# A four-layer graph network on one core: projections and sort moved beside the attention heads, searches and layer joins rearranged

## The chip, the core and the metric

The kernel runs on one core of a Trainium2 chip. A core has a matrix engine (PE, TensorE), a vector engine (DVE), an activation engine (ACT), a general-purpose engine (POOL, GpSimd) and a queue engine (SP) that issues most DMA transfers. The metric is the device time of one execution in microseconds (us). Three runs of the kernel before took 3139.11, 3139.2 and 3142.6 us; the median is 3139.2.

## The reference

There are 2708 nodes with 128 features each, and one adjacency matrix of 2708 x 2708 with random weights (each entry is present with probability 0.00148, the diagonal always). Four layers follow one another, each as `x = x + layer(relu(layernorm(x)))`:

```
layer 0: d = sum(adj, axis=1);  s = 1/(sqrt(d)+1e-8)
         (adj * s[:,None] * s[None,:]) @ (h @ W + b)
layer 1: q,k,v = (h @ W.T).reshape(128, n, 8)        # 128 heads of width 8
         a = softmax(q k^T * 128**-0.5 + 2*adj);  (a v).reshape(n, 1024) @ Wo.T
layer 2: (adj.T @ h / deg) @ Wn.T + bn + h @ Wc.T + bc, batch norm, relu
layer 3: g[i,j] = sigmoid(a[j] + b[i] + b1) * adj[i,j]
         (sum_j g[i,j] * h[i]) @ weight + bias       # a, b = h @ w1 halves
```

The reshape of layer 1 is plain: head `d` is made of consecutive pieces of the flat (n x 1024) projection, so one head covers only about 21 nodes' projections.

## The kernel before

The nodes lie in 22 row tiles of 128 rows (the last has 20). Features stay in `x_sb` through all layers.

**Layer 0 (L258 to L530)** is written in a manual schedule, that is, each engine issues in the order of the source. The three projection weights are loaded and turned first (`weight_turned`). Then come the norm of all 22 tiles, transposes into `hT`, and `fc = h @ W + b`, where the bias enters by a second matmul against a row of ones. Two passes over the adjacency follow. A row tile is loaded, ACT sums it for the degree, DVE makes `dinv` and scales `fc` (L394 to L396), PE turns 128 x 128 blocks, and PE accumulates `l_s`. The first pass (L383 to L402) goes over all tiles and finishes 8 row tiles (`stay`); the second (L493 to L518) goes over the 14 others (`gone`).

Beside both passes runs a **search** per row tile, the generator `neighbours` (L129 to L176), advanced a step at a time by `look`. It finds the 16 largest entries of each row with their columns: 8 largest in each of five segments (DVE, L134, L138), the top 16 of these 40, then a one-hot table of 16 x 40 = 640 elements (`n_hot`, DVE), its product with the column numbers (POOL, L166) and its sum over 40 (`n_col`, DVE, L174). One search is finished before the next begins. Ten tiles are searched in the first pass (`early`), twelve in the second.

**Projection and sort (L629 to L671)** form a stage of their own. Per row tile PE makes six matmuls of 128 x 512 (`qkv_ps`, six PSUM buffers), ACT and DVE copy them out in turns with a scale, and SP stores 1.6 MB to `qkv_d`. Beside it the generator `in_order` (L569) sorts the nodes by their number of neighbours: a counting sort on DVE and PE, then 22 indirect scatters on POOL (L621) that write the sorted list to `list_d`, each ordered behind the one before it. `load_wo` then loads and turns the output weight.

**The heads (L731 to L1459)** treat the softmax by an expansion in features of q and k (81 combinations), so that a head's attention is a product of moments. Heads are prepared in groups of four (`prepare`: load of `raw` from `qkv_d`, a re-ordered copy stored for the neighbour phases). The main loop (L1399 to L1445) goes over 128 heads with 6 chunks of 3 or 4 row tiles. In each chunk: `turn` transposes the next chunk's query features (PE `f_ps`, copied by ACT to `fT`), `evaluate` multiplies (PE `g_ps`), DVE makes `z` and reduces it to `o_raw`; beside it the next head's query features (`fq`, `bq`, DVE), the key features two heads ahead (`fk`, `bk`, `y`, POOL) and the next head's moments (PE `m_ps`, then `mw` on DVE, L1278) are made. All PE instructions of a chunk stand in this order in PE's queue. A further generator, `first`, advances beside the chunks through three phases: `by_node`, `sorted_rows` (which reads `list_d`) and `from_neighbours` (exact terms of the neighbours). When it is done, `normalise` and `project_out` take its turns.

**Layer 2 (L1456 to L1616)** first makes a row of inverse degrees for all partitions (`di`, then 22 pairs of a diagonal tile, a matmul `d_ps` and a copy into `diB`, L1479 to L1488). Fallback loops that run zero times here follow, then the aggregation (`pg`, L1582), batch norm and its application, which takes DVE, ACT and 22 transposes.

**Layer 3 (L1619 to L1806)** does a norm over all tiles (`norm_relu`), 22 matmuls `ab_ps` with a bias matmul each, stores the tables `gate_d` and `own_d`, and has three loops for nodes with more than 16 neighbours, which run zero times here. The gather over 22 sorted tiles ends the kernel: indirect loads on POOL (L1661), sigmoid, products, output.

## Time and profile before

| what | value |
|---|---|
| median of the runs | 3139.2 us |
| profiled execution | 3144.25 us |
| its span | 3142.5 us (1.75 us lie around it) |
| mean granted PE clock | 0.895 |
| busy share: PE, DVE, POOL, ACT | 82%, 69%, 64%, 41% |
| norm and fc | 0 to 72 us |
| first pass, second pass of layer 0 | 72 to 211, 211 to 379.7 us |
| projection and sort, until the first moments of a head | 379.7 to 539.2 us |
| heads, with their tail | 539.2 to 2661 us |
| layer 2 | 2661 to 2808.5 us |
| join of layer 2 and 3 | 2808.5 to 2896 us |
| gather | 2896 to 3142 us |

In a line of groups the columns are source line, engine, operation, output and inputs, shapes, count; then busy time and the mean nanoseconds of one; then how long the engine stood idle just before and what ended that. In a timeline line the first two numbers are start and length in us. A matmul in 32-bit floats shows as two PE instructions. A share of busy time over the whole span mixes stages, so the stretches are read one by one.

### The profile page before, as it was taken

How to read it: one execution, taken by the hardware profiler on the slowest of the kernel's cores; microseconds unless marked ns; L12 is line 12 of the kernel's file. 1: busy time of each engine (PE TensorE's matmuls, PEld its weight loads, DVE VectorE, ACT ScalarE, POOL GpSimd, SP SyncE). 2: the span in 40 equal slices, each digit the busy share in tenths (PEclk: the TensorE clock that was granted, in tenths of full speed). 3: DMA queues.
4: the chain of work that ended last, by engine and by line, in shares of the span. 5: the costliest groups of instructions: out<-in, count | busy, mean ns of one | idle time of the engine just before them, and what ended most of it. 6: DMA issues, size and time to landing. Idle time of an engine off the chain costs nothing. (4 is left out here: it accounts for less than half of the span.)

```text
span 3142.5 us, 49745 instructions
## 1 busy us (share of the span) xinstructions
PE 2587.8 (82%) x17997; PEld 2225.8 (71%) x17997; DVE 2180.7 (69%) x5130; ACT 1297.9 (41%) x3165; POOL 2009.5 (64%) x2264
## 2 busy tenths in 40 slices
PE   6478796899889999999999999999989997785144
PEld 4377543888888888888888888888889886333133
DVE  3868743777778888888888888888788885222232
ACT  3577332566644444444444444444444442112010
POOL 0211114666678988989999898989777771001775
PEclk6689897999999999999999999999999998885555
DMA  3463174778743333333433443444366642632332
GB/s 110 173 237 125 49 316 182 229 240 247 217 144 115 134 131 121 138 136 135 141 131 139 143 142 135 148 142 143 84 159 167 163 123 80 233 110 84 90 87 63
DMA packets 309521, 462.50 MB, mean 147 GB/s; under 512 B 153774, under 2 KB 229488, under 8 KB 284178
## 3 DMA queue, kind: packets, MB, share of 16 engines
q1 hardware_dynamic: 277658, 290.28, 28.8%
q0 software_dynamic: 31600, 168.86, 15.6%
q8 instruction: 147, 2.41, 0.3%
q14 instruction: 116, 0.95, 0.1%
HBM read 344.49 MB, written 114.59 MB: 146 GB/s over the span
## 5 line engine op out<-in xcount | busy, mean ns | idle before, releaser
L1306 PE MATMUL g_ps<-mw,fT 128*128 128x128 f32 x5632 | 776.0, 280 | 28.8 <-DVE mw L1278 24.8
L1296 ACT COPY fT<-f_ps 128x512 f32<-128x512 f32 (+1 forms) x768 | 419.3, 546 | 869.7 <-PE f_ps L1294 867.1
L1268 PE MATMUL m_ps<-y,fk 123*128 123x128 f32 (+1 forms) x5632 | 754.2, 280 | 0.0
L1306 PEld LDWEIGHTS g_ps<-mw,fT 128*128 128x128 f32 x5632 | 706.6, 196 | 36.5 <-DVE mw L1278 30.5
L1268 PEld LDWEIGHTS m_ps<-y,fk 123*128 123x128 f32 (+1 forms) x5632 | 703.2, 197 | 0.0
L1216 POOL TENSOR_TENSOR y<-bk,raw 128x792 f32<-128x792 f32 x256 | 415.8, 1625 | 301.4 <-ACT y L1249 291.9
L1314 DVE TENSOR_TENSOR z<-g_ps,bq 128x324 f32<-128x324 f32 (+1 forms) x768 | 355.2, 462 | 293.8 <-PE g_ps L1306 293.6
L1294 PE MATMUL f_ps<-ident,fq 128*128 128x128 f32 x2816 | 451.9, 280 | 124.7 <-DVE v_sum L860 69.7
L1294 PEld LDWEIGHTS f_ps<-ident,fq 128*128 128x128 f32 x2816 | 336.0, 143 | 214.9 <-DVE v_sum L860 73.3
L1320 DVE TENSOR_REDUCE o_raw<-z 128x36 f32<-128x324 f32 (+1 forms) x768 | 355.8, 463 | 26.4
L1216 POOL TENSOR_TENSOR fk<-bk,raw 128x352 f32<-128x352 f32 (+1 forms) x384 | 356.3, 950 | 0.1
L1216 POOL TENSOR_TENSOR fk<-raw,bk 128x352 f32<-128x352 f32 (+1 forms) x512 | 311.7, 636 | 2.9 <-ACT bk L764 2.2
L1213 DVE TENSOR_TENSOR fq<-bq,kq_ps 128x528 f32<-128x528 f32 (+1 forms) x512 | 288.1, 605 | 0.0
L972 POOL TENSOR_TENSOR c_z<-c_kv,c_q 128x1024 f32<-128x1024 f32 (+1 forms) x121 | 284.1, 2348 | 2.0 <-DMA c_kv<-kv_n,srt 1.3
L1013 PE MATMUL v_ps<-c_v,ident 128*128 128x512 f32 (+1 forms) x484 | 228.8, 595 | 6.2 <-ACT c_acc L1028 6.2
L1661 POOL DMA_INDIRECT g<-gate_d,srt x121 | 121.7, 1006 | 109.7 <-issue 109.4
L1213 DVE TENSOR_TENSOR fq<-kq_ps,bq 128x352 f32<-128x352 f32 (+1 forms) x512 | 171.9, 378 | 0.0
L155 POOL CAST n_fl<-n_ci 128x40 f32<-128x40 int32 (+1 forms) x22 | 4.8, 216 | 252.1 <-DVE n_ci L138 252.1
L978 DVE TENSOR_REDUCE c_c<-c_z 128x128 f32<-128x1024 f32 (+1 forms) x121 | 147.5, 1219 | 3.1 <-POOL c_z L972 3.1
L996 DVE TENSOR_TENSOR c_v<-c_kv,c_c 128x1024 f32<-128x1024 f32 (+1 forms) x121 | 146.7, 1212 | 0.0
L1249 ACT COPY y<-raw 128x99 f32<-128x99 f32 x256 | 95.7, 375 | 108.4 <-PE m_ps L1268 106.8
L957 POOL DMA_INDIRECT c_kv<-kv_n,srt x121 | 117.5, 971 | 22.0 <-issue 15.0
(301 smaller groups left out, 3661.1 us busy)
## 6 DMA issues: line engine op xcount, KB each, us to landing
a_nat<-in_adj_dram SPq DMA_DIRECT2D x34, 1354.0 KB
raw<-qkv_d SPq DMA_DIRECT2D x128, 275.0 KB
n_raw<-qkv_d SPq DMA_DIRECT2D x128, 275.0 KB
qkv_d<-qkv SPq DMA_DIRECT2D x21, 1600.0 KB
a<-in_adj_dram SPq DMA_DIRECT2D x21, 1354.0 KB
kv_n<-n_kv SPq DMA_DIRECT2D x16, 1408.0 KB
o_g<-o_raw SPq DMA_DIRECT2D x31, 396.0 KB
q_n<-n_q SPq DMA_DIRECT2D x16, 704.0 KB
```

Of the source, the lines that this page charges most:

```text
L972: nc.gpsimd.tensor_tensor(zs[b][:sz], kvs[b][:sz, 0, :, 0], qs[t][:sz], ALU.mult)
L978: nc.vector.reduce_sum(cs[b][:sz], zs.pop(b)[:sz], axis=AX.X)
L996: nc.vector.tensor_tensor(z[:sz], kv[:sz, 0, :, 1].rearrange("p (j c) k -> p j c k", j=2), c.rearrange("p (j c) -> p j c", j=2)[:, :, :, None]
L1013: nc.tensor.matmul(accs[t][:sz, j], ident[:sz, :sz], z[:sz, j].rearrange("p c k -> p (c k)"), start=s0 == 0, stop=s0 == ROOM[t] - 1,)
L1213: nc.vector.tensor_tensor(o, x, y, ALU.mult)
L1216: nc.gpsimd.tensor_tensor(o, x, y, ALU.mult)
L1268: nc.tensor.matmul(pms[d][:, :P], fks[d][:sz, t], ys[d, h][:sz, m * VW * B_ALL : m * VW * B_ALL + P], start=t == 0, stop=t == NT - 1,)
L1294: nc.tensor.transpose(pt[:, m], fqs[d][:, t0 + m], ident)
L1296: nc.scalar.copy(fts[d, c][:, :n], pt[:, :n])
L1306: nc.tensor.matmul(pg[:, m], ft[:, m], mws[d], start=True, stop=True,)
L1314: nc.vector.tensor_tensor(z[:, :n], pg[:, :n, : B_ALL * VW].rearrange("p t (k b) -> p t k b", k=VW), bqs[d % 2][:, t0 : t0 + n, None, :B_A ...
L1320: nc.vector.reduce_sum(ros[g][:, t0 : t0 + n, i], z[:, :n], axis=AX.X,)
```

## The change

1. **Search.** POOL adds three halving sums (320, 160 and 80 elements), so that `n_col` on DVE reduces 5 instead of 40 per neighbour. `look` may let a second search step while the first waits for its table. `early` has 12 tiles instead of 10; the searches of two tiles begin beside the norm, one step per group of four tiles. `fc` is scaled by `dinv` on POOL instead of DVE. The bias of `fc` is added by DVE, four tiles at a time. The weights are turned between the two passes and interleaved per head, with the scale folded in.
2. **Projection.** The stage is gone. `projections` makes two row tiles (8 pieces of 32 heads) before the first head, and one piece per chunk of the first 13 and a third heads: two matmuls of 128 x 384 into one PSUM tile `v_ps` of two banks (a pool with one buffer), half of it copied by ACT and half by DVE into one of two buffers, and a store of 400 KB.
3. **Sort.** `in_order` follows in the same generator, one step per chunk, with one scatter per step. `sorted_rows` waits until it is done. Its tables and the tiles of the neighbour phases lie in `area`, where the weights were. The output weight is loaded later.
4. **Layer 2.** The inverse degrees are made after layer 0, stored, and loaded to all partitions by one broadcast transfer.
5. **Layer 2 to 3.** Batch norm's application, norm, matmul and table stores go by columns of four row tiles, several columns at different steps; batch norm is one ACT instruction per column; the bias is added by DVE. The three loops become one loop that holds the others.

```diff
@@ neighbours
+        w = CAND
+        while w > SEG:
+            w //= 2
+            nc.gpsimd.tensor_tensor(
+                hot[:sz, :, :w], hot[:sz, :, :w], hot[:sz, :, w : 2 * w], ALU.add
+            )
         yield
         col = pool.tile([P, KS], FP, name="n_col")
-        nc.vector.reduce_sum(col[:sz], hot[:sz], axis=AX.X)
+        nc.vector.reduce_sum(col[:sz], hot[:sz, :, :SEG], axis=AX.X)
@@ layer 0
-            early = stay + gone[:2]
-            wT = [weight_turned(w, f"wT{i}") for i, w in enumerate((wq, wk, wv))]
+            early = stay + gone[STAY - 1 :: 2]
...
+            def look(n):
+                for _ in range(n):
+                    while found:
+                        e = found[0]
+                        if len(found) > 1 and e[1] >= 3 and e[2] and found[1][1] < 3:
+                            e[2] = False
+                            e = found[1]
+                        else:
+                            e[2] = True
+                        e[1] += 1
+                        if next(e[0], "done") != "done":
+                            break
+                        found.remove(e)
+            begun_with = [order[0], order[2]]
+            for t in begun_with:
+                i = order.index(t)
+                found.append([neighbours(t, rows[t][1], nat[i], np_, seg0, at48), 0, False])
...
-                nc.tensor.matmul(pf[:sz], ones[0:1, :sz], b0_sb, start=False, stop=True)
-                nc.scalar.copy(fc[:sz, t], pf[:sz])
+                        nc.vector.tensor_tensor(
+                            fc[:sz, t0 + a : t0 + b],
+                            pf[:sz, a:b],
+                            b0_sb[:sz, None].to_broadcast([sz, b - a, C]),
+                            ALU.add,
+                        )
+                look(1)
...
-                nc.vector.tensor_scalar_mul(fc[:sz, t], fc[:sz, t], d)
+                nc.gpsimd.tensor_scalar_mul(fc[:sz, t], fc[:sz, t], d)
...
             products(len(ready))
+            for e, (w, scale) in enumerate(((wq, C**-0.5), (wk, 1.0), (wv, 1.0))):
+                weight_turned(w, f"w{e}", e, scale)
@@ after layer 0
+    di_d = dram.tile([N, 1], FP, name="di_d")
+    di = keep.tile([P, NT, 1], FP, name="di")
...
+    store_rows(nc.sync, di_d, di)
@@ in_order
-            if t % 2:
-                yield
+            yield
@@ heads
+        def projections():
+            n = 0
+            for t, (r0, sz) in enumerate(rows):
+                rows_d = qkv_d[r0 * P : (r0 + sz) * P].rearrange("(p c) k -> p c k", c=P)
+                for c0 in range(0, C, SOME):
+                    pv = ps_v.tile([P, 2, BK], FP, name="v_ps")
+                    w = SOME // 2
+                    for j in range(2):
+                        o = (c0 + j * w) * W_OF
+                        nc.tensor.matmul(
+                            pv[:sz, j, : w * W_OF],
+                            hT[:, r0 : r0 + sz],
+                            wT[:, o : o + w * W_OF],
+                            start=True,
+                            stop=True,
+                        )
+                    yield
+                    ot = ots[n % 2]
+                    n += 1
+                    for j, copy in enumerate((nc.scalar.copy, nc.vector.tensor_copy)):
+                        copy(
+                            ot[:sz, j * w : (j + 1) * w, :W_OF],
+                            pv[:sz, j, : w * W_OF].rearrange("p (c k) -> p c k", k=W_OF),
+                        )
+                    nc.sync.dma_start(
+                        rows_d[:, c0 : c0 + SOME].rearrange("p c k -> p (c k)"),
+                        ot[:sz].rearrange("p c k -> p (c k)"),
+                    )
+                    yield
+        def made_beside():
+            yield from projections()
+            for _ in in_order(Pieces(), ps_t):
+                yield
+                yield
+            placed.append(True)
+        made = made_beside()
...
+            for _ in range(2 * 2 * C // SOME):
+                next(made)
             run(prepare(0, got))
...
                         keyed = keys(d + 2)
+                    next(made, None)
                     if c == 0 and d + 1 < D:
...
+                    next(made, None)
                     if soon and next(soon[0], "done") == "done":
@@ sorted_rows
+            while not placed:
+                yield
             load_rows(nc.sync, srt, list_d)
@@ layer 2
-            for t, (r0, sz) in enumerate(rows):
-                dg = lp.tile([P, P], FP, name="dg", tag="dg", bufs=2)
-                nc.vector.tensor_scalar_mul(dg[:sz, :sz], ident[:sz, :sz], di[:sz, t : t + 1])
-                pd = ps.tile([P, BK], FP, name="d_ps", tag="tr")
-                nc.tensor.matmul(pd[:, :sz], ones[:sz], dg[:sz, :sz], start=True, stop=True)
-                nc.scalar.copy(diB[:, r0 : r0 + sz], pd[:, :sz])
+            nc.sync.dma_start(
+                diB, di_d.rearrange("n o -> (o n)").partition_broadcast(P)
+            )
@@ layer 2 to 3
+            def column(c):
...
+                nc.scalar.activation(yc, yc, AF.Relu, bias=shift, scale=rstd)
+                yield
...
+            going, todo = [], list(range(NC))
+            while going or todo:
+                if todo:
+                    going.append(column(todo.pop(0)))
+                going = [g for g in going if next(g, "done") != "done"]
```

## The prediction

> **What bounds the kernel now.** I read the stages first (busy time per stretch), then the groups and their releasers in the projection and sort, then the timeline of one head, then that of one search. The stretches are start of layer 0's first pass, its second pass, projection, the wait after it, first 24 heads, the other heads; columns are length, busy PE, PEld, DVE, ACT, POOL, granted PE clock, DMA share, GB/s.
>
> ```profile
> 72.00:212.00 140.00, 80.88 (x522) 76.33 (x521) 106.17 (x331) 82.51 (x126) 23.72 (x50) 0.73 0.55 210
> 212.00:380.00 168.00, 126.86 (x947) 116.45 (x946) 132.13 (x416) 103.76 (x188) 29.15 (x64) 0.87 0.24 86
> 380.00:512.00 132.00, 116.88 (x272) 50.30 (x271) 54.98 (x97) 42.06 (x66) 21.96 (x25) 0.95 0.73 295
> 512.00:539.00 27.00, 11.04 (x60) 10.33 (x61) 11.20 (x28) 6.20 (x18) 20.96 (x31) 0.55 0.23 79
> 539.00:905.00 366.00, 324.59 (x2682) 315.84 (x2681) 263.80 (x638) 218.62 (x499) 239.02 (x322) 0.95 0.73 218
> 905.00:2640.00 1735.00, 1606.05 (x12492) 1455.15 (x12492) 1466.19 (x3188) 764.92 (x2042) 1499.71 (x1567) 0.98 0.42 134
> ```
> PE is the busiest engine both in the projection (116.88 of 132) and in the heads (324.59 of 366). Work taken out of the first and put beside the second finds some 40 us of idle PE there, not 116. Groups from 380 to 540:
>
> ```profile
> L652 PE MATMUL qkv_ps<-wT,hT 128*128 128x512 f32 (+1 forms) x264 | 115.3, 598 | 0.4 <-ACT hT L448 0.4
> L665 DVE TENSOR_SCALAR qkv<-qkv_ps 128x512 f32<-128x512 f32 (+1 forms) x66 | 45.6, 691 | 63.0 <-PE qkv_ps L652 63.0
> L621 POOL DMA_INDIRECT list_d<-rec,s_at x22 | 21.2, 964 | 109.9 <-DMA list_d<-rec,s_at 81.9 <-DVE s_at L618 28.1
> L840 ACT ACTIVATE sq<-raw 128x704 f32<-128x704 f32 x2 | 1.7, 842 | 23.6 <-DMA list_d<-rec,s_at 19.7 <-DVE n L843 3.9
> ```
> Projection never waits for its copies (0.4 idle); each scatter of the sort waits for the one before it, and after the last the whole core waits. A piece of a head in steady state, then the end of a search on two engines:
>
> ```profile
> 667.27 0.49 DVE L1314 TENSOR_TENSOR z<-g_ps,bq 128x324 f32<-128x324 f32 x1
> 667.79 0.49 DVE L1320 TENSOR_REDUCE o_raw<-z 128x36 f32<-128x324 f32 x1
> 667.85 0.49 PE L1294 MATMUL f_ps<-ident,fq 128*128 128x128 f32 x3
> 668.18 1.06 PE L1306 MATMUL g_ps<-mw,fT 128*128 128x128 f32 x8
> 668.20 0.94 DVE L1213 TENSOR_TENSOR fq<-bq,kq_ps 128x352 f32<-128x352 f32 x2
> 669.07 1.28 PE L1268 MATMUL m_ps<-y,fk 123*128 123x128 f32 x10
> ```
> ```profile
> 144.50 0.82 DVE L174 TENSOR_REDUCE n_col<-n_hot 128x16 f32<-128x640 f32 x1 [1.71 <-POOL n_hot L166]
> 142.93 1.53 POOL L166 TENSOR_TENSOR n_hot<-n_hot,n_fl 128x640 f32<-128x640 f32 x1 [0.82 <-DVE n_hot L160]
> ```
> In a head PE runs ahead and DVE follows; nothing in a chunk makes PE wait for DVE's tail. In a search DVE stands until POOL has multiplied.
>
> **The sum's base.** The profiled execution took 3144.25 us (span 3142.5, 1.75 around it); the median of the runs is 3139.2, so 5 us come off at the end. About 0.2%, 6 us, is what a measurement of this kernel can tell from no change.
>
> **A. Layer 0.** The instruction order of the changed program sets n_col directly behind n_hot in nearly every search, so searches hardly interleave, and DVE waits for POOL's multiply and the three halving adds. An add's price is not in the trace for 320, 160 and 80 elements; bounds are 128x352 at 0.64 to 0.95 with 128x88 at 0.36 (sum 1.3 to 1.8), and I take 1.55. The reduction falls from 0.82 to about 0.25 (a 128x4 from 128x88 took 0.24). In the first pass two fc scalings of 0.29 go to POOL. A search there: 12.57 + 1.55 - 0.57 - 0.58 = 12.97; in the second pass 12.45 + 0.98 = 13.43. The first two searches stand beside the norm, the third begins when ACT has reached the fifth tile's degree, about 90; ten more end at 219, and the second pass begins near 225 (before: 222). The weights are now turned there, about 10 us of copies, and ten searches instead of twelve take 134: 369, with the tail 372.5 instead of 379.7. **A = -7**; from -35 (searches that do overlap) to +35 (norm and searches in each other's way, the adds at 1.8, weight turning bare).
>
> **B. Projection taken out of the way.** Before: 379.7 to the first weighted moments (L1278) at 539.24, 159.5 us. After: two row tiles in 8 pieces. A piece has 4 PE instructions of 128x384; 115.3/264 = 0.437 for 512, so 0.32 each, 1.28, then ACT's copy 0.48 (636 x 384/512), DVE's 0.52, hand-overs 0.2: 2.45, in all 19.6. The last store lands in about 4 (scatters land in 3.2 to 5.8); from the first load of heads to 539.24 took 23.1. Together 46.7: **B = -113**, range -95 to -120. The sort no longer stands there, its 19.7 us wait included.
>
> **C. The other 80 pieces, one per chunk of the first 13.3 heads.** Work: 80 x 1.28 = 102 us of PE, copies of 0.48 on ACT and 0.52 on DVE, a 400 KB store each. What matters is where they stand. The PSUM tile v_ps has one buffer. In the order lists PE does per chunk v_ps, f_ps, g_ps, m_ps; DVE does z, o_raw, features, then the copy of v_ps; the next v_ps waits for that copy on DVE, z waits for g_ps, which on PE is behind v_ps. That closes a ring through both engines that the kernel before does not have. Per head, from the rows above: v_ps 24 x 0.32 = 7.7; f_ps 22 x 0.15 = 3.3; g_ps 44 x 0.1325 = 5.8; z 4 x 0.49 + 2 x 0.41 = 2.8; o_raw 2.8; features between z and copy 3.7 (bq 0.56, fq 0.67, 0.24, 1.31, 0.94); copies 6 x 0.52 = 3.1; twelve hand-overs of about 0.1 (POOL began 0.14 after DVE's n_hot, DVE 0.04 after POOL's) 1.2. Sum 30.4. Moments, fk, mw and the group's reductions follow the copy or stand beside it, and cost nothing while the ring is longer. PE would then be busy 21 of 30, and its clock could fall: stretches with PE busy 89, 76 and 58% had 0.95, 0.87 and 0.73, but these contain long waits; a 20 us stretch of heads at 80% had 0.91. At 0.91 the 16.8 us of PE in the ring grow by 0.7; at 0.79 (the stages' line at 65%) by 3.4. I take 0.7: 31.1 per head. Before, heads here take 15.35 (61.4 for four, three at 13.0 to 13.7 and one with the next group's preparation at 19.3 to 21.6). **C = 13.33 x (31.1 - 15.35) = +210.** Lower end +88: PE alone, with 15 of the 102 soaked up by the preparation stalls. Upper end +270: the preparation's 8 us per four heads not covered (+28) and the lower clock (+36).
>
> On that clock a page has a rule. The Trainium skill, "TensorE: Matmul & The Clock Gate", section "HAM oscillation — how this bites in real kernels", says the clock falls back when PE idles longer than about 3.4 us. An estimate from that page: idle gaps of about 2 us per chunk would cost no clock, and the total would be 9 us lower; the stages' rows here, with their 0.73 and 0.87, cannot settle it.
>
> **D. Sort beside heads 13.3 to 19.** One scatter per chunk on POOL, each waiting for the one before: 4.87 us apart in the trace, against chunks of 15.35/6 = 2.55. 22 x 2.32 = 51, less POOL's lead of about 6 (its y waits 100.8 us for ACT in 300): **D = +45.** Behind the waiting scatter stand y and fk on POOL, and PE's m_ps waits for those. Ends: +5 if landings fall to the unloaded 3.2 and POOL's lead covers them, +80 if they take 5.8. The list is complete near head 19, before the sorted phase wants it (21.7), so that costs nothing unless the order moves.
>
> **E. Layer 2.** The degree row built on PE and DVE (2662.3 to 2673.1) becomes a broadcast load with work beside it: **-8** (-10 to 0); pg, at 0.43 us per PE instruction, sets the stage and hides the load.
>
> **F. Layer 2 to 3.** 2808.5 to the first gather at 2896.1. The 44 bias matmuls (17.2 busy) go and batch norm, norm, matmul and stores run by columns: 69 us to about 49, **-20**; three loops become one nest, where their barriers left DVE idle 7.0 and ACT 16.0 before: I take **-8**. Together -28 (-15 to -38). Gather work is the same.
>
> **Sum.** -7 - 113 + 210 + 45 - 8 - 28 = +99: 3243, on the median's scale 3238; I say 3240.
>
> **A rule that would say otherwise.** "Perfetto Trace Analysis", section "Optimization Strategy", advises interleaving regimes whose most-contended engine changes. An estimate by it, with the projection hidden whole, would make C zero and the total about 3028. The stages' rows above show the same engine in both regimes.
>
> **The rivals.**
> 1. *PE alone counts* (no change): the copies keep pace, as they did in the projection stage (0.4 idle). C = +102: 3131. Against it: one v_ps buffer and the copy behind z. 0.12.
> 2. *Faster*: copies and scatters both find room. For it: a preparation head leaves 6 to 8 us of idle PE, POOL waits a third of the time. C = +88, D = +5: 3077. The mechanism is PE's idle time in the heads; it decides once a head with projection takes less than 23.6 us (chunk 3.9), where C + D is 156. 0.13.
> 3. *Ring plus layer 0*: halving adds on POOL in every search with nothing interleaved, A = +35: 3280, with its spread 3240 to 3330. 0.15.
> My own case, the ring through one PSUM buffer, has 0.60 and 3165 to 3310 of its own.
>
> **How the numbers follow.** Faster: 0.13 + half of 0.12 + 0.05 from my case's low tail = 0.24; same 0.05; slower 0.71. The range leaves out rival 2 and a few hundredths above: 3105 to 3315.
>
> **What would show it.** C: heads 0 to 13 at 29 to 33 us each, v_ps waiting for DVE's copy in nearly every chunk, granted clock near 0.9; wrong if they take under 24. D: list_d rows on POOL waiting for list_d, with y late behind them, and heads near 15 to 19 slower than 15.35. A: n_col waiting about 3.2 us for POOL; second pass ends near 372. B: first L1278-type product near 419. E, F: last head to first gather about 36 us shorter. What makes me wrong above all: an order of copies that lets PE run past the ring, or heads that absorb the projections in idle time I counted as needed.

## The result and the profile after

The changed kernel takes 3285.3 us (median of four runs, 3276.0 to 3287.9) against 3140.9 us of the kernel before beside it: a ratio of 1.0452, with a 95% interval of 1.0427 to 1.0476. It is 4.5% slower. The profiled execution took 3284.09 us, its span 3282.3, 139.8 us longer than the span before. (The gather's 21 us in this difference are no work of the change, as e5 shows below; on one and the same chip, in e0, the two medians lie 152.8 us apart.) The table follows the same events through both traces (offsets in us from the start of the span) and sets the difference of each stretch beside the step of the prediction that spoke of it.

| stretch | before | after | difference | predicted |
|---|---|---|---|---|
| start to the first projection matmul (end of layer 0) | 379.7 | 381.7 | +2.0 | A: -7 |
| to the first moments `mw` of a head | 159.5 | 58.9 | -100.7 | B: -113 |
| to head 14's `mw` | 212.4 | 459.0 | +246.6 | C: +210 |
| heads 14 to 24 | 153.3 | 187.1 | +33.8 | D: +45 |
| heads 24 to 106 | 1360.9 | 1357.1 | -3.8 | none |
| heads 106 to 127 | 362.3 | 395.8 | +33.5 | none |
| last `mw` to the last add of the head output | 32.7 | 30.2 | -2.5 | none |
| to the end of batch norm's statistics (`bn_mv`) | 147.4 | 144.9 | -2.5 | E: -8 |
| to the first gather of layer 3 | 87.8 | 42.4 | -45.4 | F: -28 |
| gather | 246.4 | 225.3 | -21.1 | none |

Five rows carry nearly all of it. The stretches of the changed kernel (length, then busy time of PE, PEld, DVE, ACT, POOL, granted PE clock, DMA share, GB/s):

```profile
380.00:425.00 45.00, 21.87 (x51) 9.68 (x48) 12.36 (x44) 8.74 (x22) 5.50 (x14) 0.71 0.32 114
425.00:850.00 425.00, 292.94 (x1707) 231.49 (x1708) 176.36 (x415) 149.97 (x349) 136.87 (x176) 0.93 0.54 177
850.00:965.00 115.00, 85.55 (x628) 73.95 (x626) 73.78 (x173) 53.02 (x118) 54.06 (x64) 0.94 0.67 203
965.00:1030.00 65.00, 43.72 (x327) 42.04 (x328) 32.17 (x81) 26.08 (x60) 46.64 (x58) 0.78 0.43 134
1030.00:2790.00 1760.00, 1605.75 (x12446) 1455.32 (x12446) 1479.97 (x3167) 773.45 (x2062) 1506.57 (x1612) 0.97 0.42 134
```

Between 425 and 850, where the projection pieces stand beside heads, no engine is busy more than 69% of the time (PE, 292.94 of 425). The kernel before had PE at 89% in both of its stages. Work that was bound by one engine has become bound by none: that is how a ring looks in this view. The groups of the changed kernel between 420 and 850 name it (line, operation, count, busy time and mean ns, then idle time just before and what ended it):

```profile
L1189 PE MATMUL v_ps<-area 128*128 128x384 f32 x295 | 125.2, 551 | 121.1 <-DVE qkv L1200 109.4 <-DVE mw L1392 11.7
L1200 DVE COPY qkv<-v_ps 128x384 f32<-128x384 f32 x73 | 40.1, 549 | 20.5 <-ACT qkv L1200 20.5
L1200 ACT COPY qkv<-v_ps 128x384 f32<-128x384 f32 x73 | 35.7, 489 | 23.8 <-DMA qkv_d<-qkv 23.8
L1428 DVE TENSOR_TENSOR z<-g_ps,bq 128x324 f32<-128x324 f32 (+1 forms) x73 | 34.1, 468 | 215.2 <-PE g_ps L1420 215.2
```

PE waits 109.4 us for DVE's copy of `v_ps`, and DVE waits 215.2 us for PE's `g_ps`: each stands for the other. One turn of it in the timeline of the changed kernel (start, length, engine and line, in brackets the idle time before and its releaser):

```profile
607.95 0.55 DVE L1200 COPY qkv<-v_ps 128x384 f32<-128x384 f32 x1
...
608.64 1.53 PE L1189 MATMUL v_ps<-area 128*128 128x384 f32 x4 [1.50 <-DVE qkv L1200]
...
610.01 0.60 PE L1408 MATMUL f_ps<-ident,fq 128*128 128x128 f32 x4
...
610.44 1.06 PE L1420 MATMUL g_ps<-mw,fT 128*128 128x128 f32 x8
...
611.54 0.50 DVE L1428 TENSOR_TENSOR z<-g_ps,bq 128x324 f32<-128x324 f32 x1 [1.97 <-PE g_ps L1420]
...
612.07 0.49 DVE L1434 TENSOR_REDUCE o_raw<-z 128x36 f32<-128x324 f32 x1
612.48 0.56 DVE L1327 TENSOR_TENSOR bq<-kq_ps,raw 128x88 f32<-128x88 f32 x3
612.95 0.55 DVE L1200 COPY qkv<-v_ps 128x384 f32<-128x384 f32 x1
```

Copy, `v_ps`, `f_ps`, `g_ps`, `z`, `o_raw`, features, copy: 5.00 us from one copy to the next, one after the other on two engines. Read a ring in this way: follow one tile from its reader back to its next writer, and look whether any instruction in between runs beside another.

The sort, in the timeline of the changed kernel:

```profile
963.03 0.96 POOL L675 DMA_INDIRECT list_d<-rec,area  x1 [5.20 <-DMA list_d<-rec,area]
964.01 1.61 POOL L1330 TENSOR_TENSOR y<-bk,raw 128x792 f32<-128x792 f32 x1
967.07 1.01 POOL L675 DMA_INDIRECT list_d<-rec,area  x1 [1.45 <-DMA list_d<-rec,area]
968.11 0.95 POOL L1330 TENSOR_TENSOR bk<-raw 128x88 f32<-128x88 f32 x3
968.50 0.71 DVE L1327 TENSOR_TENSOR fk<-bk,kq_ps 128x528 f32<-128x528 f32 x1 [13.55 <-POOL bk L1330]
...
973.45 1.11 PE L1408 MATMUL f_ps<-ident,fq 128*128 128x128 f32 x4 [14.77 <-DVE v_sum L911]
```

A scatter waits 5.20 us on POOL for the scatter before it; `y` and `bk` stand behind; DVE stops 13.55 us for `bk`, and PE 14.77 us for DVE.

Last, a stretch for which the prediction had no term. Near head 106 of the changed kernel:

```profile
2457.36 0.87 POOL L1330 TENSOR_TENSOR fk<-bk,raw 128x352 f32<-128x352 f32 x1
...
2457.88 12.03 DVE L1160 TENSOR_TENSOR area<-area,r_rs 128x704 f32<-128x704 f32 x1
2458.16 1.65 POOL L1330 TENSOR_TENSOR y<-bk,raw 128x792 f32<-128x792 f32 x1
...
2466.37 2.79 POOL L1330 TENSOR_TENSOR fk<-bk,raw 128x528 f32<-128x528 f32 x3
2469.83 0.69 DVE L1159 RECIPROCAL r_rs<-area 128x88 f32<-128x88 f32 x1
2470.56 0.89 DVE L1160 TENSOR_TENSOR area<-area,r_rs 128x704 f32<-128x704 f32 x1
```

The same product of `normalise` takes 12.03 us once and 0.89 the next time. Two more took 9.59 and 5.55 us; in the profile of before the longest was 3.62. It has no wait in front of it: it runs long, while POOL issues one instruction after another. POOL's row ends at 2469.16 (2466.37 + 2.79), and the product at 2469.91, 0.75 us later, about the time it takes undisturbed.

That is not the usual case. In the kernel before, the product also starts inside unbroken rows of POOL, but mostly waits for one instruction only. Near head 121 of before (the first row is two sums on POOL, the second of which ends at 2518.32):

```profile
2514.65 3.67 POOL L1100 TENSOR_TENSOR r_raw<-r_raw,r_more 128x792 f32<-128x792 f32 x2
...
2517.27 1.80 DVE L1107 TENSOR_TENSOR r_more<-r_raw,r_rs 128x704 f32<-128x704 f32 x1
2518.29 2.51 POOL L1100 TENSOR_TENSOR r_both<-r_both 128x792 f32<-128x792 f32 x1
```

Here the product ends at 2519.07, 0.75 us after the POOL instruction that was under way, and POOL's next sum takes 2.51 us; beside no such product it took 1.9. So the two engines do hold each other up, in both directions. In the changed kernel's three long cases POOL got the next turn every time; what decides that is not shown.

### The profile page after: what moved, and what is told of

Read it like the earlier page. It is cut to its first block, busy times and chain, and to the rows that moved or that the text cites. A ratio compares the mean times of both kernels' runs of the same rounds, so it can differ in the third digit from the quotient of the medians.

```text
span 3282.3 us, 49573 instructions
## 1 busy us (share of the span) xinstructions
PE 2570.0 (78%) x17952; PEld 2228.1 (68%) x17952; DVE 2171.9 (66%) x5074; ACT 1275.9 (39%) x3087; POOL 2054.3 (63%) x2362
## 5 line engine op out<-in xcount | busy, mean ns | idle before, releaser
L1025 POOL TENSOR_TENSOR area<-c_kv,area 128x1024 f32<-128x1024 f32 (+1 forms) x121 | 283.8, 2346 | 2.7 <-DMA c_kv<-kv_n,srt 2.0
L1189 PE MATMUL v_ps<-area 128*128 128x384 f32 (+1 forms) x352 | 155.8, 571 | 141.6 <-DVE qkv L1200 127.4
L1066 PE MATMUL v_ps<-area,ident 128*128 128x512 f32 (+1 forms) x484 | 228.8, 595 | 5.9 <-ACT c_acc L1081 5.9
L1189 PEld LDWEIGHTS v_ps<-area 128*128 128x128 f32 (+1 forms) x352 | 65.3, 206 | 189.9 <-issue 143.8
L1031 DVE TENSOR_REDUCE c_c<-area 128x128 f32<-128x1024 f32 (+1 forms) x121 | 147.4, 1218 | 3.8 <-POOL area L1025 3.8
L1049 DVE TENSOR_TENSOR area<-c_kv,c_c 128x1024 f32<-128x1024 f32 (+1 forms) x121 | 146.5, 1211 | 0.0
L1837 POOL DMA_INDIRECT g<-gate_d,srt x121 | 120.8, 999 | 36.9 <-issue 34.4
L1330 POOL TENSOR_TENSOR bk<-raw 128x88 f32<-128x88 f32 x384 | 125.1, 354 | 29.1 <-DMA raw<-qkv_d 28.9
```

Of the source, the lines that this page charges most:

```text
L1025: nc.gpsimd.tensor_tensor(zs[b][:sz], kvs[b][:sz, 0, :, 0], qs[t][:sz], ALU.mult)
L1031: nc.vector.reduce_sum(cs[b][:sz], zs.pop(b)[:sz], axis=AX.X)
L1066: nc.tensor.matmul(accs[t][:sz, j], ident[:sz, :sz], z[:sz, j].rearrange("p c k -> p (c k)"), start=s0 == 0, stop=s0 == ROOM[t] - 1,)
L1189: nc.tensor.matmul(pv[:sz, j, : w * W_OF], hT[:, r0 : r0 + sz], wT[:, o : o + w * W_OF], start=True, stop=True,)
L1330: nc.gpsimd.tensor_tensor(o, x, y, ALU.mult)
```

## The experiments

All kernels below compute the whole reference. Each was compared with the kernel before on its own chip; those medians were 3160.0 (e1, e2, e3, e5_tail_only), 3133.1 (e0, e6, e7, e8), 3131.4 (e5_again, e9, e10) and 3132.8 us (e11b), so totals are compared as ratios, and the stretches within a trace in us.

| kernel | median us | ratio to before, 95% |
|---|---|---|
| the changed kernel, again (e0) | 3285.9 | 1.0463 (1.0433 to 1.0494) |
| e1: copies directly behind the matmuls | 3222.7 | 1.0189 (1.0147 to 1.0231) |
| e7: e1, and both copies on ACT | 3188.5 | 1.0167 (1.0144 to 1.0190) |
| e2: half as many scatters per chunk | 3366.2 | 1.0638 (1.0595 to 1.0680) |
| e3: no halving sums | 3282.6 | 1.0372 (1.0330 to 1.0413) |
| e5: before, with parts 4 and 5 alone | 3102.3; 3085.3 | 0.9805 (0.9767 to 0.9843); 0.9838 (0.9806 to 0.9870) |
| e6: e5, the product's second operand in PSUM | 3128.8 | 0.9991 (0.9971 to 1.0011) |
| e8: a projection stage kept, other parts in | 3108.5 | 0.9921 (0.9899 to 0.9944) |
| e9: e5, the product on POOL | 3067.6 | 0.9801 (0.9779 to 0.9822) |
| e10: a stage kept, the product on POOL | 3045.4 | 0.9728 (0.9711 to 0.9745) |
| e11b: the changed place, all mends in | 3136.6 | 1.0007 (0.9991 to 1.0023) |

### e1 and e7: is it the ring?

e1 moves the copies of a piece to stand directly behind its matmuls, ahead of `z` on DVE, so that DVE's tail is no longer between two pieces:

```diff
@@ projections (e1)
                             stop=True,
                         )
-                    yield
                     ot = ots[n % 2]
...
                         ot[:sz].rearrange("p c k -> p (c k)"),
                     )
                     yield
+                    yield
```

> Changed kernel, but a piece's two copies and its store are issued directly behind its matmuls, at the start of the chunk, so that DVE's copy stands before z and not behind z, o_raw and the features. Ring theory: v_ps of the next chunk finds its buffer free, PE no longer waits for DVE, a head costs PE's own 13.0 + 6 x 1.56 = 22.4 us, with hand-overs 22 to 25 instead of 33.2; 13.7 heads x about 9.7 = 133 us less, total 3130 to 3190. Rival, two store buffers (ACT's copies waited 23.8 us for stores) or the bare amount of work bind: heads stay at 30 or more, total above 3240.

Measured: heads 0 to 13 at 27.55 us each (33.25 in the changed kernel), ratio 1.0189. The order of the copies is worth 5.7 us a head, so the ring was there; but the heads do not fall to 22 to 25. The groups of e1 between 440 and 790:

```profile
L1189 PE MATMUL v_ps<-area 128*128 128x384 f32 (+1 forms) x304 | 125.4, 539 | 65.7 <-DVE qkv L1199 64.8
...
L1199 DVE COPY qkv<-v_ps 128x384 f32<-128x384 f32 (+1 forms) x75 | 41.8, 557 | 155.0 <-ACT qkv L1199 154.7
L1199 ACT COPY qkv<-v_ps 128x384 f32<-128x384 f32 (+1 forms) x75 | 35.9, 478 | 184.9 <-DMA qkv_d<-qkv 94.3 <-issue 48.5 <-PE v_ps L1189 32.2
```

Read from below: ACT waits 94.3 us for the stores to empty one of the two `qkv` buffers, DVE waits 154.7 us for ACT, PE 64.8 us for DVE. With the ring open, the next thing that is late is the store buffer. Why DVE waits for ACT's copy before its own is not shown (both write one tile); e7 gives both copies to ACT, to see whether that wait or the buffers hold the heads.

```diff
@@ projections (e7, on top of e1)
-                    for j, copy in enumerate((nc.scalar.copy, nc.vector.tensor_copy)):
+                    for j, copy in enumerate((nc.scalar.copy, nc.scalar.copy)):
```

> Changed kernel with a piece's copies directly behind its matmuls, both halves copied by ACT. With one half on DVE a head took 27.5 us, not the 22 to 25 expected; DVE's copies then waited 154.7 us for ACT's, and ACT's 94.3 for stores. If DVE's waiting in front of z binds: heads of 23 to 24, total some 50 below that run, near 3170. If the two store buffers (or ACT) bind: heads of 27 or more, total 3220 or above.

Measured: 26.35 us a head, ratio 1.0167. The groups of e7 in the same stretch:

```profile
L1189 PE MATMUL v_ps<-area 128*128 128x384 f32 (+1 forms) x308 | 127.4, 540 | 61.5 <-ACT qkv L1199 61.5
L1199 ACT COPY qkv<-v_ps 128x384 f32<-128x384 f32 (+1 forms) x156 | 67.0, 481 | 161.0 <-DMA qkv_d<-qkv 89.2 <-issue 37.2 <-PE v_ps L1189 27.1
```

Taking DVE out of it was worth 1.2 us a head, net of ACT's second copy; in the totals the two ratios cannot be told apart. ACT still waits 89.2 us for the stores, and PE 61.5 us for ACT: the store buffers, through ACT, are what the trace names now. Neither a third store buffer nor a second `v_ps` was tried at this place, so what the heads would take without these waits is open.

### e2: is it POOL's queue?

```diff
@@ made_beside
             for _ in in_order(Pieces(), ps_t):
                 yield
                 yield
+                yield
+                yield
```

> Changed kernel, but the sort takes a step every second chunk, so one scatter per two chunks (5.1 us of head work against 4.87 between two scatters). Queue theory: POOL no longer stands in front of y, bk and fk waiting for the last scatter; heads 14 to 24, which were 33.8 us longer than before, lose 20 to 30 of it, total 3254 to 3264. Rival, the sort's own DVE and PE steps and the 22 issues of 1 us cost it: less than 10 us gained, total above 3274.

Measured: heads 14 to 24 in 159.1 us, against 187.1 in the changed kernel and 153.3 before. That part held: with time to land between two scatters the queue is nearly free. (Five of the 22 scatters come after head 24; heads 24 to 28 took 69.4 us with them and 67.8 in the changed kernel.) What POOL waited for its own scatters, in the view of the tile `list_d` (us, times), in the changed kernel:

```profile
  DMA list_d<-rec,area: 29.7, 13
```

And e2, in the same view:

```profile
  DMA list_d<-rec,area: 9.9, 4
```

But the total went to 1.0638, against 1.0452 and 1.0463 of the changed kernel: some 60 us the other way, and the expectation of it was missed. The list is loaded at 1076.6 instead of 1050.3, near head 25 instead of head 22, past the point where `sorted_rows` wants it. 74 us instead of 30 then pass from the last `mw` to the last add: work that stands beside chunks and begins later runs out of chunks, as I read it. I had named the bound (21.7) in the prediction and did not apply it to my own experiment. That is not all, since heads 24 to 106 take 1413.0 instead of 1357.1. What PE waited there (us in total, times, longest), in the changed kernel and in e2:

```profile
PE f_ps L1408 <- DVE v_sum L911: 51.6, 21, 2.8
PE f_ps L1410 <- DVE v_sum L911: 114.2, 21, 6.3
```

Once per group of four heads PE waits 3 us longer for a sum on DVE, and the granted clock there is 0.95 instead of 0.98. Which of the shifted work stands in front of that sum was not followed up.

### e3: what do the halving sums cost?

```diff
@@ neighbours
-        w = CAND
-        while w > SEG:
-            w //= 2
-            nc.gpsimd.tensor_tensor(
-                hot[:sz, :, :w], hot[:sz, :, :w], hot[:sz, :, w : 2 * w], ALU.add
-            )
...
-        nc.vector.reduce_sum(col[:sz], hot[:sz, :, :SEG], axis=AX.X)
+        nc.vector.reduce_sum(col[:sz], hot[:sz], axis=AX.X)
```

> Changed kernel without POOL's three halving sums; n_col reduces 640 elements on DVE again. Theory of step A: the wait for POOL before n_col falls from 3.4 us to 1.7, the sum grows from 0.23 to 0.82, so each search is about 1.1 us shorter; 20 searches that stand in the passes make 15 to 25 us, total 3259 to 3269. Rival, the passes are set by ACT's degrees and by PE: 5 us or less, total 3279 or more.

The group of the reduction between 100 and 380, in the changed kernel:

```profile
L180 DVE TENSOR_REDUCE n_col<-n_hot 128x16 f32<-128x80 f32 (+1 forms) x19 | 4.5, 235 | 64.7 <-POOL n_hot L175 64.7
```

And in e3:

```profile
L174 DVE TENSOR_REDUCE n_col<-n_hot 128x16 f32<-128x640 f32 (+1 forms) x19 | 15.5, 818 | 29.6 <-POOL n_hot L166 29.6
```

The reduction is shorter by 11 us in 19 searches, the wait in front of it longer by 35. Layer 0 ends at 358.8 without the sums instead of 381.7: they cost 23 us there. Layer 0's other edits were worth 21 us (17 in e10 below, which ends layer 0 at 362.4), which the sums ate. (e3's span, 3285.2, holds a gather of 247 us, of which below, so the expected total, 3259 to 3269, was missed; by the last heads it is ahead of the changed kernel by 19 us, inside the 15 to 25 that were expected.)

### e5: the tail alone

The kernel before, with the inverse degrees by broadcast and the join of layers 2 and 3 by columns:

```diff
@@ before: after layer 0
+    di_d = dram.tile([N, 1], FP, name="di_d")
+    di = keep.tile([P, NT, 1], FP, name="di")
...
+    store_rows(nc.sync, di_d, di)
@@ before: layer 2, join and layer 3 as in the changed kernel
...
```

> Kernel before with only the degree row by broadcast and the new way from layer 2 to layer 3 (parts 4 and 5). By the prediction's terms E and F: -36, 3105. By the slices of the two profiles (last sum of layer 1 to first gather 47.9 us shorter, gather 21.1 shorter): -69, 3072, if the shorter gather belongs to this part; -48, 3093, if it belongs to another part or to chance.

> Kernel before with parts 4 and 5 only, once more, as the base of the next two on their chip. First run: ratio 0.9805 to the kernel before, two products of 14.6 and 11.2 us. If the long products come from the order of instructions they are here again at the same places (0.978 to 0.984); if from chance, they differ.

Measured: ratio 0.9805 and, on another chip, 0.9838. From the last add of the heads to the first gather 235.2 us became 182.7 and 182.7: -52.5, in both. So a part of the change is a gain by itself. Two things came beside it. First, the long products are here too (14.62 and 11.14 us) though no line of the heads is changed; heads 106 to 127 took 385.7 and 383.3 us instead of 362.3. They come again at the same places on another chip, so they belong to the program and not to chance. (The changed kernel's three come again in e0, e1, e3 and e7, within 0.1 us; in e2, where the work is shifted, the longest are 9.47, 5.60 and 5.53.) What in the program moved them is not settled. Second, the gather took 246.7 us on the first chip and 225.0 on the second, with the same kernel. ACT's group in the gather, in the first run of e5:

```profile
L1862 ACT COPY sup<-sup_ps 128x128 f32<-128x128 f32 (+1 forms) x22 | 5.7, 259 | 91.4 <-remote 68.7 <-PE sup_ps L1858 16.5 <-issue 6.1
```

And in the second:

```profile
L1862 ACT COPY sup<-sup_ps 128x128 f32<-128x128 f32 (+1 forms) x22 | 5.5, 249 | 22.0 <-PE sup_ps L1858 22.0
```

The -21.1 us of the gather in the table above is therefore no work of the change: the kernel before shows 60.4 us of the same "remote" in its profile. It goes with the chip: the four kernels profiled on the chip of e1, e2, e3 and e5's first run had gathers of 246.4 to 248.1 us, the eight on three other chips 225.0 to 226.3, with the old heads and the new. Why that chip is slower there remains open.

### e0, e6 and e9: what are the long products?

> The changed kernel unaltered, on the chip that runs its variants, as their base. In its first profile the gather (from the first gathered row to the end) took 225.3 us, in the kernel before and in four variants 246 to 248. If that was the change, 225 again and a total near 3285; if it was that execution or that chip, 246 or 247 and a total near 3305.

The changed kernel on another chip has the same products long: 12.01, 9.61, 5.62 us, and a gather of 226 us. The product reads two operands from SBUF while POOL works. e6 takes one of them out of SBUF, e9 takes the product off DVE:

```diff
@@ normalise (e6, on top of e5)
-            rs = sm.tile([P, NT, GRP], FP, name="r_rs")
+            while adding:
+                yield 1
+            rs = sum_bank()[:, : NT * GRP].rearrange("p (t i) -> p t i", i=GRP)
@@ normalise (e9, on top of e5)
-            rs = sm.tile([P, NT, GRP], FP, name="r_rs")
+            rs = sm.tile([P, NT, GRP], FP, name="r_rs", bufs=6)
...
-            nc.vector.tensor_tensor(
+            yield SOON
+            nc.gpsimd.tensor_tensor(
```

> Kernel before with parts 4 and 5 (as in the run of these alone), and in normalise the reciprocals lie in PSUM instead of SBUF, so that DVE's product reads one operand from SBUF and one from PSUM. In the run of parts 4 and 5 alone two of these products took 14.64 and 11.15 us instead of 0.89, each ending when POOL's row of products ended. Theory of the shared port: none above 1.5 us, heads 105 to 127 some 20 us shorter, total 20 to 30 below that run, 3072 to 3085. Rival, DVE was slow for another reason (addresses, the transfers that ran then): products above 5 us remain and the total stays at 3100.

> Kernel before with parts 4 and 5, and normalise's product on POOL (the reciprocal stays on DVE, its tile has six buffers). With the reciprocals in PSUM the long products were gone, but the output projection then waited for that PSUM tile and the last heads and the tail became about 45 us longer. Here nothing shares a tile: if the port was what cost the last 20 heads, 20 to 25 us below the run of parts 4 and 5 alone; POOL gets 32 x 1.7 = 54 us more work there. Rival, POOL is then late with y and the heads wait for it: no gain or a loss.

The groups of e6 between 2270 and 2650:

```profile
L726 PE MATMUL c_c<-woT,o_both 128*128 128x128 f32 x117 | 27.0, 423 | 34.4 <-DVE r_more L1116 34.4
...
L1116 DVE TENSOR_TENSOR r_more<-r_raw,c_c 128x704 f32<-128x704 f32 x18 | 16.0, 887 | 0.6
```

With the reciprocals read from PSUM no product took more than 0.89 us, though ten of the 21 began while a POOL instruction ran. POOL's work stayed as it was, so the second operand in SBUF is shown to be a condition; that POOL is the other party rests on the two timelines above, where the product ends 0.75 us after POOL's instructions and POOL's own become longer. But the bank is the one that `project_out` accumulates in, and PE now waits 34.4 us for the product to leave it; heads 106 to 127 took 386.6 us, 70 us went from the last `mw` to the last add, and the ratio is 0.9991. The mend of one wait made another: the expectation of the total was missed, that of the mechanism held. The product in the view of its tile, in e5 (second run; duration ns min/median/max, first and last start):

```profile
L1114 DVE TENSOR_TENSOR r_more<-r_raw,r_rs x21: 891/1669/14621, 2274.4 to 2660.5; 128x704 f32<-128x704 f32 x21
```

And in e9:

```profile
L1115 POOL TENSOR_TENSOR r_more<-r_raw,r_rs x21: 1398/1413/1496, 2278.2 to 2635.8; 128x704 f32<-128x704 f32 x21
```

On POOL it takes 1.40 to 1.50 us, and heads 106 to 127 take 344.0 us: 39 less than with it on DVE, and 18 less than before. Half of that comes back behind them, where 51.7 us instead of 32.6 pass from the last `mw` to the last add: from head 106 to that add e9 takes 395.7 us, 20 less than e5, and as long as the kernel before (395.0). So the move takes away what the long products cost, and no more. By the median e9 is 17.8 us faster than e5 on the same chip, though the intervals of their ratios just overlap.

### e8, e10 and e11b: the place of the projection

e8 and e10 keep a projection stage ahead of the heads, with the changed kernel's 384-wide pieces and scaled weights, six PSUM buffers, three store buffers and the sort beside it. Layer 0 is the changed one without the halving sums. e8 has the product as in e6, e10 as in e9. e11b leaves the projection where the change put it and has every mend at once: copies as in e7, no halving sums, the product on POOL. (Its first form, e11, with six buffers for the reciprocals as in e9, did not fit into SBUF, where a pool of 6 KB per partition found 4.84 KB left, and gave no time; e11b keeps the reciprocals in the unused end of the group's own tile.)

```diff
@@ the changed kernel: heads (e8, e10)
-        made = made_beside()
+        made = iter(())
@@ ahead of the heads (e8, e10)
+            ots = [op.tile([P, C, QKV], FP, name=f"qkv{i}") for i in range(3)]
...
+            sort = in_order(so, ps)
...
+                    n += 1
+                    if n % 2:
+                        nc.scalar.copy(to, got_)
+                    else:
+                        nc.vector.tensor_copy(to, got_)
+                        next(sort, None)
```

> What the runs so far speak for, together: projection and sort as a stage of their own again (six PSUM buffers, copies in turns), no halving sums, the rest of the new layer 0 and parts 4 and 5 kept, normalise's reciprocals in PSUM. Layer 0 without halving put the first head 27 us earlier than with it, which had been level with before; so some 20 to 27 below the run with parts 4 and 5 and the reciprocals in PSUM: 3048 to 3062. If layer 0's gain was only the overlap with the row tiles, it equals that run.

> The kernel with the projection stage kept, no halving sums, parts 4 and 5, and normalise's product on POOL instead of the reciprocals in PSUM. That one had its first head 21 us earlier than the kernel before, and lost about 40 us in the last heads and the tail. Expected: 12 to 20 us below the previous kernel of this call, ratio to the kernel before near 0.965. Rival, the late load of the output weight and the lists in the large tile eat the head start: equal to it.

> The changed kernel with the projections still beside the heads, but with all that helped: a piece's copies directly behind its matmuls and on ACT, no halving sums, normalise's product on POOL (its reciprocals in the unused end of the group's own tile). Against the same kernel with projection and sort as a stage of their own (ratio 0.9728) it tells what the place of the projections alone costs. By the profiles: 13.7 heads at 26.7 instead of 15.4 make +155, the stage's 160 us shrink to about 58, -101, the sort's scatters +33, so +80 to +100: ratio 0.998 to 1.006, near 3130 to 3150. If the projections now fit into the heads, within 20 us of the stage.

Measured: e8 0.9921, 20 us below e6 as expected of layer 0, but not the 3048 to 3062 expected in all, since the PSUM tile's wait of e6 is in it (heads 106 to 127 in 393.8 us). e10 takes 3045.4 us, ratio 0.9728: faster than both kernels. e11b is 1.0007, no different from before, inside its 0.998 to 1.006. Between e10 and e11b almost only the place of projection and sort differs:

| stretch | e10 | e11b | difference |
|---|---|---|---|
| start to the first `mw` | 518.2 | 405.8 | -112.4 |
| to head 14's `mw` | 210.9 | 377.0 | +166.1 |
| heads 14 to 24 | 150.5 | 188.8 | +38.3 |
| heads 24 to 106 | 1355.3 | 1354.3 | -1.0 |
| heads 106 to 127 | 341.2 | 342.3 | +1.1 |

The place, with the buffers that go with it (one `v_ps` and two store buffers against six PSUM and three store buffers), costs 92 us up to the last heads and 90 in the spans. How much of it more buffers would save is not tested. The stages of e10 (columns as above) show what it is competing with:

```profile
380.00:512.00 132.00, 104.35 (x328) 60.73 (x327) 57.04 (x118) 42.94 (x96) 35.08 (x44) 0.89 0.77 296
512.00:539.00 27.00, 26.62 (x223) 25.97 (x223) 16.92 (x43) 15.37 (x38) 24.19 (x34) 0.95 0.22 67
539.00:905.00 366.00, 324.19 (x2667) 313.09 (x2665) 268.93 (x641) 215.92 (x496) 246.63 (x326) 0.96 0.76 222
```

In the stage a piece costs 112.4/80 = 1.40 us with the sort beside it for nothing; beside heads it costs 166.1/80 = 2.08 and the sort another 38 us. PE is the engine in demand on both sides (104 of 132, 324 of 366), so there was little idle time to put it in.

## Why the prediction was right and where it was wrong

The direction and the range held: 3285 lies in 3105 to 3315. The likeliest time, 3240, was 45 us low (+99 forecast, +139.8 in the spans, +144 in the medians). That it came so near is partly luck: 33.5 us in heads 106 to 127 had no term at all, while the gather (-21.1) and F (17 more than forecast) happen to give 38 back. By its steps:

**C, the ring, was right in mechanism and mis-sized in one term.** Heads 0 to 13 took 33.25 us (29 to 33 were named, 31.1 taken), `v_ps` waits for DVE's copy, and e1 takes 5.7 us a head away by moving only that copy. The term that was too small is the price of `v_ps`: 1.28 us per piece, from matmuls that stood back to back in the projection stage (0.437 each at 512 wide). In the ring the four instructions are 1.53 us in the turn shown and at the median, and 125.2 us over 73.75 pieces, 1.70 each, in the mean. The difference of 0.42 over 80 pieces is 34 us, and C's miss is 36.6. Of the 0.42, 0.25 is what they take after a wait and not back to back: a price out of a saturated stage does not hold there. The other 0.17 comes from eleven of 74 pieces that took 1.80 to 2.91 us, each of them in a stretch where the granted clock stood at 0.50. (0.03 of the 0.25 is rounding in the sum: 0.437 at 512 wide is 0.328 at 384, not 0.32.)

**The clock was a bound too many.** The prediction gave 0.79 as the low end, from the stages' line at PE busy 65%, and took 0.91. The heads with projections ran at 0.93 with PE busy 69%: the line through the stages does not hold for them. The Trainium skill, "TensorE: Matmul & The Clock Gate", section "HAM oscillation — how this bites in real kernels", asks for no PE idle gaps above about 3.4 us. The trace agrees in part. Between 437 and 850 the clock stood at 0.50 for 51 us, in eleven stretches: eight go with the eight PE gaps of 3.73 to 5.79 us, and three with gaps of 2.2 us, of which four others left no mark; shorter gaps, as the 1.50 us in the turn shown, left none. But from 388.9 to 409.4 it stood at 0.50 too, behind gaps of 1.79 and 2.89 us, with PE busy for 14.64 of the 20.5 us. The gaps that I put at about 2 us a chunk were 1.5 with a few of 4 to 6, so that the estimate of no clock cost at all did not hold either.

**B: -100.7 instead of -113, one term again.** The first pieces have nothing beside them. The second waits until 389.6 for DVE's copy of the first, and five of the eight run at a clock of 0.50, where the four instructions take 2.93 us and a piece 4.13 us instead of 2.45. From 381.7 to 414.5 the eight take 32.8 us where 19.6 were forecast: 13.2, against a miss of 12.3. (The 3.2 to 5.8 us that stood for a store's landing are distances between scatters in the trace of before; the store's own landing is not shown there.)

**D: +33.8 instead of +45.** The queue was as forecast, down to the `y` behind the scatter. The scatters stand 4.11 us apart (930.0 to 1016.4) instead of the 4.87 of the projection stage: 22 x (4.11 - 2.55) = 34. POOL's lead, for which 6 us came off, bought next to nothing.

**A: +2.0 instead of -7, wrong in sign.** The halving sums were priced about rightly: 0.98 us for a search of the second pass, 1.3 measured in e3 (35.1 - 11.0 over 19). The rest of layer 0 was taken too well: the first pass ends 7 us later than before (217.7 against 210.9) where 3 were forecast, and the second gains 5 where 10 were. The third rival, layer 0 at +35, fell with it; its total of 3280 comes close for other reasons, and is no confirmation.

**E and F.** F gave -45.4 against -28 (-15 to -38). e5 shows the same 43 us from `bn_mv` to the first gather (2815.2 to 2857.9) with the heads of before, so it is the join's own. The low term is that of the columns: from `bn_mv` to the last copy into the tables 70 us became 34, where 69 and 49 stood in the sum. From that copy to the first gather 17.6 became 8.8, which is the -8 of the loops. E gave 2.5 of the 8 in the changed kernel, but 140.0 against 147.4, 7.4, in e5; why less of it is left here is open.

**What no step had: heads 106 to 127, +33.5.** The sum put this stretch at nothing. The products of `normalise` were in no part of the diff that I followed, since their operation did not change. The Trainium skill, "SBUF — State Buffer", section "Who interferes with whom", says that a vector instruction with two inputs in SBUF contends with a GpSimd instruction that reads SBUF, and one with a single SBUF input does not. The trace agrees on both (up to 14.62 us, and 0.89 with one input in PSUM). It shows one thing more: in these long cases the product does not lose one POOL instruction but a whole unbroken row of them. The longest in the changed kernel starts while one of 0.87 us is under way and ends after that one and the 13 behind it. The three long products have 24.5 us over 0.89 each; all 21 together took 50.7 us against 33.1 before. Behind them stands `mw` on DVE, for which PE waited 26.4 us in these heads against 8.2 before, and for the adds that empty `c_c` it waited 18.6 against 9.0; that is 28 of the 33.5, and the rest is not traced.

**The rivals.** That PE alone counts (3131) fell to the 109.4 us wait of `v_ps`. The faster one asked for heads under 23.6 us; with copies first, then on one engine, they stayed at 27.55 and 26.35, and the best form of that place ended at 1.0007. The estimate of 3028 by the advice to interleave regimes fell as well, for the reason that the stages' rows gave: the advice, as the prediction gives it, is for regimes with different busiest engines, and here it is PE in both.

## What to carry to other kernels

Before work is moved beside other work, ask which engine is idle where it goes, and follow every single-buffered tile from its last reader to its next writer through the queues in between: a reader behind instructions that wait for what stands behind the next writer closes a ring, and its length is the sum of both engines' work in it. Price each moved instruction as it will stand (cold, after a wait, alone), not as it stood in a full stage. When a stretch slows down that the change does not touch, look for one instruction with a maximum far above its median, and at what the neighbouring engine does while it runs.

## What the runs showed of the hardware that was not expected

- A DVE product of 128x704 with both operands in SBUF took 0.89 us or up to 14.62 us, without a wait in front of it, while POOL issued instructions back to back. In the kernel before it mostly waited for the one POOL instruction under way (1.67 to 1.83 us), and POOL's next one was longer (2.51 us for 1.9); in the long cases it waited for a whole row. The same places came long on two chips. With one operand in PSUM it took 0.89 us throughout.
- The same kernel's gather took 246.7 us on one chip and 225.0 us on another, and so did all gathers of these two chips within 2 us; the difference lies in ACT's "remote" and "issue" waits (68.7 and 6.1 us against none), and no line of the kernel explains it.
- The granted clock stayed at 0.93 with PE busy 69% in short pieces, and stood at 0.50 for 20.5 us over the first pieces of the projection, where PE was busy for 14.64 of them and never idle for more than 1.2 us at a time, behind gaps of 1.79 and 2.89 us.
